# Identity products in TensorE's idle stretches, and one thread's wide keys and values early, in a planned four-block transformer kernel

## The chip, the cores and the metric

The kernel runs on one core of one Trainium2 chip. The metric is the time of one execution on the device in microseconds (us). All data are fp32. A core has TensorE (PE: matrix products and transposes, results into PSUM), VectorE (DVE), ScalarE (ACT), GpSimd (POOL) and SyncE (SP), which here only issues DMAs. In a trace one fp32 product is two instructions, each with its own load of the stationary operand; a transpose is one.

## The reference

Eight sequences of 128 tokens with 256 features, `x`, pass through four blocks. `ctx` has the same shape and is what the cross attentions look at. Cut to what matters:

```python
# block 0: 16 heads of 16 features, keys and values from ctx, mask over keys
x = x + attn(LN(x), ctx) @ cproj_w + cproj_b
x = x + gelu(LN(x) @ fc_w + fc_b) @ proj_w + proj_b              # 256 -> 1024 -> 256
# block 1: queries from x, keys and values from ctx and x together (256 keys)
a = attn(x, concat(ctx, x)) @ out_w + out_b + x
x = x + gelu(RMS(a) @ mlp_w1 + mlp_b1) @ mlp_w2 + mlp_b2
# block 2, twice: 16 wide heads of 128 features, one learned extra key and value
for i in (1, 2):
    q, k, v = LN(x) @ wq, ctx @ wk, ctx @ wv                      # 256 -> 2048 each
    x = x + softmax([q k', q bias_k'] / sqrt(128)) @ [v, bias_v] @ wo + bo
x = x + gelu(LN(x) @ w_fc1 + b_fc1) @ w_fc2 + b_fc2
# block 3: self attention with a causal mask, cross attention to ctx, MLP
x = x + attn(LN(x), LN(x)) @ w_ao + b_ao
x = x + attn(LN(x), ctx) @ w_co + b_co
x = x + gelu(LN(x) @ w1 + b1) @ w2 + b2
```

Only block 2's keys and values are wide, and they depend on nothing but `ctx` and weights.

## The kernel before, in words

**Threads.** The eight sequences are worked on in four threads, T0 to T3, of two sequences (256 tokens) each. Each runs through the four blocks by itself: ten stages with weights of their own, namely a0, m0, a1, m1 (blocks 0 and 1; a is attention, m is MLP), the two wide attentions, m2, then a4, a5, m3 (block 3). T2 starts when T0 has left m1 (`front_done`), T3 when T1 has left it and T0 has left the wide attentions (`wide_done`). So at the beginning only T0 and T1 run.

**Planner.** The instruction order of every engine is written by a planner, class `Plan`, when the program is built. Every step is a Python generator started by `spawn` with an urgency (lower goes first). A step asks for an engine with `op(engine, function)`, waits for an `Event`, or takes buffers from a `Slots` counter. `Plan.run` keeps a clock of its own: when it holds an engine to be free, `_choose` takes the waiting request of lowest urgency, runs its function (which records the instructions) and adds a modelled duration from `_weight`. On the chip each engine runs its list in that order, and semaphores make it wait for what it really needs. `Clock` models TensorE's clock: windows of 3413 ns, full speed in the next window if the last was busy enough, half if not. Every instruction is recorded by the wrapper `Engine`, so all of them bear one line in a trace, and groups are told apart by their tiles.

**Names of tiles.** `mm` (2 banks), `tl` (2 banks) and `sc` (4 banks) are PSUM: `mm` takes projections and MLPs, `tl` transposes, wide scores and weighted values, `sc` the scores of narrow heads. `w` is a weight tile of 512 KB (11 buffers, at most four in use by a thread), `kb` a 128x256 tile for wide keys, wide queries and hidden MLP units (20), `vw` wide values (4), `bv` the wide value bias (2), `t` softmax weights, `xn` a normalised input, `hT` its transpose, `q`, `k`, `v`, `mp`, `tm`, `attnT` the parts of narrow attention, `ident` the 128x128 identity.

**Wide attention.** `wide_attention(T, i)` takes the norm, then the four groups of four heads one after the other with `group(T, i, hg, hT, hT_in)`. In a group, `keys` projects `ctx` into four `kb` tiles (two blocks of four products of 128x256, evicted by ACT or DVE with a bias), `queries` does the same with the normalised input, `values` projects each sequence of `ctx` into a `vw` tile (two products of 128x512, evicted by DVE with the bias `bv`, which `value_bias` makes from two DMAs of 256 KB and a subtraction on POOL). Then, for each sequence, come scores, softmax and the product with `wo` (`after_scores`).

**Weights.** `loader(T)` asks for a thread's weights in the fixed order of `weight_list` as its four slots come free; the DMAs are issued by SP in the order in which the planner reaches them.

**Urgencies.** Each stage has a constant, and each thread three offsets added to it, one for the stages before the wide attentions, one for those, one for the stages after: `LATE = [(0.0, 0.0, 2.3), (3.0, 0.1, 4.5), (2.3, 1.3, 2.6), (1.3, 0.8, 2.3)]`.

Of the kernel before, what the change touches and what calls it, by code (L numbers as in the profile page):

```python
# [58 lines left out]

class Event:  # L60
# [14 lines left out]
class Plan:  # L75
# [12 lines left out]
    def __init__(self):  # L88
        self.now = 0
        self.seq = 0  # L90
        self.events = []
        self.asked = []
        self.until = {e: 0 for e in self.SEEN}
        self.weight, self.shared, self.wrote = 0, False, []
        self.both_until = {"DVE": 0, "POOL": 0}
        self.clock = Clock()
        self.log = []
        self.table = None
        self.dma_until = 0
        self.live = {}  # L100
# [76 lines left out]
    def run(self):  # L177
        self.now = max(self.until.values())
        while self.events or self.asked:
# [3 lines left out]
            for eng in self.until:  # L183
                if self.until[eng] <= self.now:
                    got = self._choose(eng)
                    if got:
                        _, a, (_, ns, f, lat, table), load = got
                        self.asked.remove(a)
                        self.weight, self.shared, self.wrote = ns, False, []
# [6 lines left out]
                        self.log.append((eng, self.now, end - self.now, f.__qualname__.replace("four_blocks.<locals>.", "").replace("<locals>.", "")))  # L196
# [14 lines left out]
class Clock:  # L211
# [4 lines left out]
    def __init__(self):  # L216
        self.t, self.busy, self.fast = 0.0, 0.0, False
        self.end = self.W

# [9 lines left out]
    def work(self, start, ns):  # L229
        self._go(start, False)  # L230
        while ns > 1e-6:
            speed = 1.0 if self.fast else 0.5
            d = min(self.end - self.t, ns / speed)
            self._go(self.t + d, True)
            ns -= d * speed
        return self.t


def _weight(eng, name, args, kw):
# [6 lines left out]
    if eng == "PE":  # L246
# [8 lines left out]
        return max(224, 1.685 * cols), False  # L255
# [29 lines left out]
class Engine:  # L285
# [5 lines left out]
    def __getattr__(self, name):  # L291
        f = getattr(self._eng, name)

        def call(*args, **kw):
# [3 lines left out]
            if eng != "PE" and any(x.tensor is y.tensor and x.offset == y.offset for x in aps[1:] for y in plan.wrote):  # L298
# [4 lines left out]
            plan.shared |= both  # L303
            return f(*args, **kw)  # L304
# [21 lines left out]
def four_blocks(ctx: ExitStack, tc: tile.TileContext, a: dict, out: bass.AP):  # L326
# [40 lines left out]


# [47 lines left out]
    class Thread:  # L416
        def __init__(self, h, b0, nb):
# [10 lines left out]
            self.late = 0.0  # L428

# [42 lines left out]
    def loader(T):  # L472
        for name, shape, pieces in weight_list():
# [7 lines left out]
    def all_then(evs, then):  # L481
        for e in evs:
            yield e
        plan.set(then)
# [32 lines left out]
    def each(*rs):  # L517

        for e in [spawn(asks(r), 0.0) for r in rs]:
# [137 lines left out]
    def product(ops, take):  # L657
# [5 lines left out]
        return spawn(taken(p, take), 0.0, Plan.SEEN["PE"])  # L663
# [6 lines left out]
    def mlp(T, name, src, e, w, b, b1, func, table, adds, to):  # L670
        hT, hT_in = yield from normed(T, src, e, w, b, adds, 2.0 + T.late)
# [22 lines left out]
        yield spawn(first(), 3.0 + T.late)  # L694
# [11 lines left out]
        yield spawn(second(), 3.0 + T.late)  # L706
# [45 lines left out]
    def attention(T, name, norm, ns, own_keys, scale, qb, kb_, vb, mask_of, masks, to):  # L752
# [7 lines left out]
        hT, hT_in = yield from normed(T, *norm, 1.0 + late)  # L760
# [8 lines left out]
        between = spawn(fill(v, 1.0 if by_key else 0.0), 2.0 + late)  # L769
# [11 lines left out]
        biases_in = spawn(cols_then(biases), 2.0 + late)  # L781
        mask_in = spawn(mask_of(mask, k, hs, ks, biases_in), 2.0 + late)
# [63 lines left out]
        k_in = [spawn(keys(s, *src), 2.0 + late) for s, src in enumerate(sources)]  # L846
        yield weight(T, f"{name}qo")
        q_in = spawn(queries(), 1.5 + late)
        v_in = [spawn(values_of(s, *src), 2.5 + late) for s, src in enumerate(sources)]
# [17 lines left out]
        yield spawn(out(), 1.0 + late)  # L867

    def by_keys(T, ns, scale, mask, masks, q, k, v, v_in, vb, attnT):
# [4 lines left out]
        def item(b, c0, n):  # L874
# [94 lines left out]
            e1 = spawn(even_part(1), 0.5 + late)  # L969
# [18 lines left out]
        for b in range(T.nb):  # L988
            for c0 in range(0, NC, 2 // ns):
                done.append(spawn(item(b, c0, 2 // ns), 0.5 + late))  # L990
# [3 lines left out]
    def by_pairs(T, ns, scale, mask, masks, q, k, v, v_in, vb, attnT):  # L994
# [4 lines left out]
        def item(b):  # L999
# [17 lines left out]
            soft = [spawn(softmax(s[:, r], b, r, mn, sm, ts), 1.0 + late) for r in range(4)]  # L1017
# [26 lines left out]
        def values(b, soft, ts, turn, next_turn):  # L1044
# [3 lines left out]
            for r in range(4):  # L1048
# [14 lines left out]
                evs.append(spawn(out_of(pt, pts[:, r]), 1.0 + late, Plan.SEEN["PE"]))  # L1063
# [23 lines left out]
        for b in range(T.nb):  # L1087
            soft, ts = yield from item(b)
            nxt = Event()
            done.append(spawn(values(b, soft, ts, turn, nxt), 0.5 + late))  # L1090
# [25 lines left out]
    def wide_attention(T, i):  # L1116
        hT, hT_in = yield from normed(
            T, T.x, 1e-5, f"L2_ln{i}_scale", f"L2_ln{i}_offset", [(T.x, T.x, f"L2_bo{i}")], 0.5)
# [6 lines left out]
    def group(T, i, hg, hT, hT_in):  # L1125

        n = f"l{i}{hg}"
        ks, qs, vs = [], [], []
        bv = new(wpool, [P, 512], "bv", bufs=2)
        bv_in = spawn(value_bias(bv, i, hg), 1.0)  # L1130
        sb = new(act, [P, 4], "sb", bufs=6)
        late, nb, nt = T.late, T.nb, T.nt
        v_in = [Event() for _ in range(nb)]

        def keys():
# [17 lines left out]
            drop(T)  # L1153
            for e in ends:
                yield e

        def queries():
            yield weight(T, n + "q")
            yield hT_in
            s = P ** -0.5  # L1160
            yield op("POOL", lambda: nc.gpsimd.tensor_scalar(
                sb, col(f"L2_bq{i}", 4 * hg, 4), s, None, ALU.mult))
            ends = []
            for m in range(0, 4, 2):
                yield (kb_slots, 2)
                two = [kb(), kb()]
                qs.extend(two)

                def take(p, two=two, m=m):
                    b = col(f"L2_bq{i}", 4 * hg + m, 2)  # L1170
                    yield from each(*(either(
                        lambda j=j: nc.scalar.activation(
                            two[j][:, :nt], p[:, j * nt : (j + 1) * nt], AF.Identity, bias=sb[:, m + j : m + j + 1], scale=s),
                        lambda j=j: nc.vector.tensor_scalar(
                            two[j][:, :nt], p[:, j * nt : (j + 1) * nt], b[:, j : j + 1], s, ALU.add, ALU.mult),
                    ) for j in range(2)))
                ends.append((yield from product(proj(T.w[n + "q"], hT, (m, m + 1)), take)))
# [231 lines left out]
```

## Time and profile before

| | |
|---|---|
| median of 3 runs | 1224.16 us (1221.81 to 1225.23) |
| profiled execution | 1224.51 us |
| its span, first to last instruction | 1222.7 us |
| TensorE busy | 1146.0 us, 94% of the span |
| DVE, ACT, POOL busy | 759.8, 563.1, 341.9 us |
| mean granted TensorE clock | 0.975 |
| moved by DMA | 145.57 MB |

The profile gives each engine's busy time, then the span in 40 slices of 30.6 us in which a digit is the busy share in tenths, with the TensorE clock that was granted (in tenths of full speed), then DMA queues, the chain of work that ended last, and the costliest groups of instructions. A line of windows gives the same for any stretch of time; a line of the timeline gives a start, a busy time, the group, and in brackets the idle time before it and what ended it. A row's mean duration is longer than the pitch at which such instructions follow each other, since products are pipelined.

### The profile page before, as it was taken

The page shows a single profiled execution, that of the slowest core. Times are in us where ns is not written, and L with a number is a line of the kernel's source. Part 1 is how long each engine was busy: PE and PEld are TensorE (multiplying, and loading weights), DVE is VectorE, ACT ScalarE, POOL GpSimd, SP SyncE. Part 2 cuts the span into 40 slices and gives each one's busy share as a digit, 9 for nine tenths or more (in the row PEclk, how much of TensorE's full clock was granted, in tenths as well). Part 3 has the DMA queues.
Part 4 walks back from the last instruction along what each step waited for, and adds up shares of the span by engine and source line. Part 5 has one row for each costly group of instructions (what it writes and reads, how often), then busy time and mean ns, then how long its engine had stood idle before and what let it go on. Part 6 is the DMA issues. An engine that isn't in the chain of part 4 may idle for free.

```text
span 1222.7 us, 21753 instructions
## 1 busy us (share of the span) xinstructions
PE 1146.0 (94%) x8224; PEld 936.9 (77%) x8224; DVE 759.8 (62%) x1955; ACT 563.1 (46%) x1418; POOL 341.9 (28%) x397
## 2 busy tenths in 40 slices
PE   6699799999999999999999999999999999989868
PEld 4577577787877877868877888888887888877647
DVE  6665668625773546758668564444637756788771
ACT  4244445344533334527346443335333634968652
POOL 3021111111112212116424120221212522676660
PEclk9699899999999999999999999999999999989879
DMA  9133142444434443553434325454436245321400
GB/s 296 42 92 106 36 130 90 138 123 138 118 120 140 146 150 101 147 171 99 121 92 136 106 91 187 141 159 139 143 121 179 75 149 156 111 81 44 131 1 18
DMA packets 107320, 145.57 MB, mean 119 GB/s; under 512 B 6736, under 2 KB 66256, under 8 KB 107216
## 3 DMA queue, kind: packets, MB, share of 16 engines
q1 hardware_dynamic: 107216, 144.18, 38.4%
q8 instruction: 65, 1.06, 0.3%
q14 instruction: 39, 0.32, 0.1%
HBM read 143.11 MB, written 1.05 MB: 118 GB/s over the span
## 4 chain that ended last, share of the span: by engine, by line
PE 78%; DVE 11%; ACT 6%; DMA 3%; issue 1%; POOL 1%; SPq 0%; ACTq 0%; DVEq 0%; POOLq 0%
PE mm L304 56%; PE tl L304 17%; PE sc L304 5%; DVE t L304 1%; ACT t L304 1%; ACT L304 1%; DVE mp L304 1%; DVE rz L304 1%; DMA w<-in_L_k_w 1%; DVE q L304 1%; DVE tm L304 1%; ACT pt L304 1%; DVE mn L304 1%; DVE x L304 1%; ACT q L304 1%
## 5 line engine op out<-in xcount | busy, mean ns | idle before, releaser
L304 PE MATMUL mm<-hT,w 128*128 128x256 f32 x1216 | 289.8, 385 | 9.3 <-ACT kb L304 2.0
L304 PEld LDWEIGHTS mm<-hT,w 128*128 128x128 f32 x1216 | 226.7, 192 | 47.5 <-issue 5.9
L304 POOL TENSOR_TENSOR t<-t,sm 128x512 f32<-128x512 f32 x128 | 131.8, 1043 | 337.9 <-DVE sm L304 206.5
L304 PE MATMUL mm<-ctxT,w 128*128 128x256 f32 x608 | 145.4, 384 | 9.6 <-DMA w<-in_L_k_w 9.5
L304 PE MATMUL mm<-w,ctxT 128*128 128x512 f32 (+1 forms) x352 | 144.0, 539 | 1.9 <-ACT kb L304 0.9
L304 PEld LDWEIGHTS mm<-ctxT,w 128*128 128x128 f32 x608 | 113.0, 192 | 26.7 <-issue 9.8
L304 DVE TENSOR_TENSOR x<-mm,x 128x256 f32<-128x256 f32 (+1 forms) x96 | 49.0, 510 | 131.2 <-PE mm L304 130.9
L304 POOL TENSOR_TENSOR x<-x,row 128x512 f32<-128x512 f32 x40 | 50.8, 1270 | 272.3 <-ACT xn L304 180.4
L304 PE MATMUL mm<-w,at 128*128 128x256 f32 x512 | 121.5, 381 | 1.3 <-PE mm L304 1.0
L304 PE MATMUL mm<-w,kb 128*128 128x256 f32 x512 | 117.8, 380 | 0.0
L304 PEld LDWEIGHTS mm<-w,at 128*128 128x128 f32 x512 | 95.0, 190 | 19.0 <-issue 3.7
L304 PEld LDWEIGHTS mm<-w,kb 128*128 128x128 f32 x512 | 95.5, 190 | 14.1 <-issue 1.4
L304 ACT ACTIVATE t<-t,mn 128x128 f32<-128x128 f32 x256 | 99.0, 391 | 8.4 <-DVE mn L304 6.5
L304 PE MATMUL tl<-ident,t 128*128 128x128 f32 x512 | 79.9, 287 | 16.6 <-POOL t L304 9.8
L304 PEld LDWEIGHTS mm<-w,ctxT 128*128 128x128 f32 x352 | 63.4, 192 | 39.3 <-issue 32.1
L304 POOL TENSOR_TENSOR t<-t,mask 128x512 f32<-128x512 f32 x64 | 80.4, 1280 | 46.3 <-DVE t L304 44.2
L304 PEld LDWEIGHTS tl<-ident,t 128*128 128x128 f32 x512 | 63.3, 147 | 34.2 <-POOL t L304 18.7
L304 ACT ACTIVATE t<-t 128x516 f32<-128x516 f32 x64 | 40.5, 633 | 101.9 <-DVE t L304 101.8
L304 ACT ACTIVATE kb<-mm,cols 128x256 f32<-128x256 f32 x128 | 53.2, 471 | 71.2 <-PE mm L304 70.9
L304 ACT ACTIVATE at<-tl,cols 128x128 f32<-128x128 f32 x204 | 58.2, 368 | 54.8 <-PE tl L304 54.5
L304 POOL TENSOR_TENSOR bv<-bv,bb 128x512 f32<-128x512 f32 x32 | 40.6, 1270 | 115.2 <-DMA bb<-in_L_bias_v 94.6
L304 DVE TENSOR_SCALAR kb<-mm,cols 128x256 f32<-128x256 f32 x61 | 28.9, 481 | 66.6 <-ACT kb L304 64.8
(117 smaller groups left out, 1798.6 us busy)
## 6 DMA issues: line engine op xcount, KB each, us to landing
w<-in_L_wk SPq DMA_DIRECT2D x32, 512.0 KB, 4.3
w<-in_L_wq SPq DMA_DIRECT2D x32, 512.0 KB, 3.7
w<-in_L_wv SPq DMA_DIRECT2D x32, 512.0 KB, 3.7
w<-in_L_wo SPq DMA_DIRECT2D x32, 512.0 KB, 3.4
w<-in_L_mlp_w SPq DMA_DIRECT2D x16, 512.0 KB, 3.9
bv<-in_L_bv SPq DMA_DIRECT2D x32, 256.0 KB, 4.6
bb<-in_L_bias_v SPq DMA_DIRECT2D x32, 256.0 KB, 5.7
w<-in_L_w_fc SPq DMA_DIRECT2D x16, 512.0 KB, 3.9
```

The source lines that it names most:

```text
L304: return f(*args, **kw)
```

## The change

**Identity products.** When the planner finds TensorE free with no request for it, and its model says that the clock is slow or that TensorE was busy for less than 0.55 of the last 3413 ns, it records one product of the identity with itself (128x128) into a free `mm` or else `tl` bank. Nothing reads the result. It can do so again as soon as that product has ended in its model.

**Early keys and values.** `keys` and `values` move out of `group` into a function of their own, `keys_values`. For T0, the groups (1, 0) and (1, 1), that is eight heads of the first wide attention, are started at the beginning of `blocks`, with an offset of their own; `group` picks up the result. `loader` takes their four weights after the first two of T0's list. In a group that isn't early, the queries are now started before the keys, and the values are started when the keys' requests are done.

**Urgencies and prices.** The stages' constants move into a table `U` with new values, and `LATE` now has ten offsets for each thread, one for each stage. The planner's price of a product goes from `max(224, 1.685 n)` to `max(225, 1.7 n)` ns for n columns. It now finds by name, not by object, that an instruction reads what the one before it on its engine wrote, and then adds the delay that it already had for that. `count` and `log` are bookkeeping.

By the built order of instructions, 64 identity products are in the new program: 17 before the first other product, 6 and 4 in the first attentions of T0 and T1, 9 between scores of T1's a1 and the transposes of T0's norm for m1, 12 before the transposes of T0's first wide norm, and 16 among the last stages (2, 2, 9 and 3). The other products are the same in number.

```diff
+WARM = True
+AHEAD = [[(1, 0), (1, 1)], [], [], []]
+U = {'take': 0.33, 'taken': -1, 'norm': 0.36, 'mask': 1.35, 'k': 2.41, 'q': 1.92, 'v': 2.5, 'by key': 0.5, 'softmax': 2.4, 'weights': 0.74, 'pairs': 0.3, 'out': 0.94, 'mlp norm': 0.75, 'mlp 1': 3.6, 'mlp 2': 2.28, 'wide norm': -1, 'wide k': 3.49, 'wide q': 4.0, 'wide v': 4.5, 'wide s': 1.19, 'wide': -0.42, 'ahead': 2.48}
+LATE = [(2.3, -0.18, 0.84, -0.88, 1.83, -0.17, 2.53, 1.2, 3.66, 1.59), (7.76, 6.61, 5.49, 5.66, 1.7, 0.2, 4.52, 3.1, 7.31, 7.88), (1.86, 2.79, 2.79, -0.1, 2.14, -1, 4.58, 4.78, 5.62, 1.93), (0.03, 1.63, -0.02, 0.92, 0.05, 2.99, -1, 0.16, -1, -1)]
...
                     got = self._choose(eng)
+                    if not got and eng == "PE" and self.idle_work and (self.events or self.asked):
+                        self.weight = 0
+                        if self.clock.lazy(self.now) and self.idle_work():
+                            self.until[eng] = self._end(eng)
...
+    def lazy(self, now):
+
+        self._go(now, False)
+        self.spans = [(a, b) for a, b in self.spans if b > now - self.W]
+        return not self.fast or sum(b - max(a, now - self.W) for a, b in self.spans) < 0.55 * self.W
...
-        return max(224, 1.685 * cols), False
+        return max(225, 1.7 * cols), False
...
-            if eng != "PE" and any(x.tensor is y.tensor and x.offset == y.offset for x in aps[1:] for y in plan.wrote):
+            if eng != "PE" and any(x.tensor.name == y.tensor.name and x.offset == y.offset for x in aps[1:] for y in plan.wrote):
...
+    def idle_work():
+
+        for slots, tag in ((mm, "mm"), (tl, "tl")):
+            if slots.free:
+                nc.tensor.matmul(bank(tag)[:, :P], lhsT=ident, rhs=ident, start=True, stop=True)
+                return True
...
     def loader(T):
-        for name, shape, pieces in weight_list():
+        names = list(weight_list())
+        first = {f"l{i}{hg}{x}" for i, hg in AHEAD[T.h] for x in "kv"}
+        ahead = [x for x in names if x[0] in first]
+        names = [x for x in names if x[0] not in first]
+        for name, shape, pieces in names[:2] + ahead + names[2:]:
...
-        k_in, q_in = spawn(keys(), 4.0 + late), spawn(queries(), 4.0 + late)
+        k_in = spawn(keys(), U["wide k"] + step_back)
+        spawn(all_then([k_in], None, lambda: spawn(values(), U["wide v"] + step_back)), 0)
+        return ks, vs, k_in, v_in
...
+        q_in = spawn(queries(), U["wide q"] + late)
+        ks, vs, k_in, v_in = T.ahead.pop((i, hg), None) or keys_values(T, i, hg, late)
         yield k_in
-        spawn(values(), 4.5 + late)
         yield q_in
...
+        for i, hg in AHEAD[h]:
+            T.ahead[i, hg] = keys_values(T, i, hg, LATE[h][0] + U["ahead"])
...
+    plan.idle_work = idle_work if WARM else None
```

## The prediction

> **What bounds the kernel now.** I read the page first, for the engine that is full and where it isn't, then windows over the span, then TensorE's timeline in the windows that stick out. T0 to T3 are the four threads.
>
> ```profile
> span 1222.7 us, 21753 instructions
> PE 1146.0 (94%) x8224; PEld 936.9 (77%) x8224; DVE 759.8 (62%) x1955; ACT 563.1 (46%) x1418; POOL 341.9 (28%) x397
> ...
> PE   6699799999999999999999999999999999989868
> ...
> PEclk9699899999999999999999999999999999989879
> ...
> PE 78%; DVE 11%; ACT 6%; DMA 3%; issue 1%; POOL 1%; SPq 0%; ACTq 0%; DVEq 0%; POOLq 0%
> ```
>
> TensorE is busy 1146.0 of 1222.7 us and carries 78% of the chain of waits. The slices that are not 9 lie in the first five and the last five, and the granted clock dips in the same ones. The windows give their size:
>
> ```profile
> 0.00:176.00 176.00, 142.78 (x1330) 113.47 (x1330) 108.61 (x313) 73.23 (x123) 28.48 (x59) 0.91 0.38 119
> 176.00:1101.00 925.00, 905.59 (x6087) 743.43 (x6088) 577.55 (x1457) 420.11 (x1047) 252.82 (x281) 1.00 0.42 128
> 1101.00:1222.70 121.70, 97.67 (x809) 80.04 (x807) 73.62 (x185) 69.74 (x249) 60.58 (x58) 0.90 0.15 48
> ...
> 30.00:56.00 26.00, 16.25 (x208) 13.51 (x208) 15.24 (x25) 5.51 (x6) 0.00 (x0) 0.61 0.09 32
> 138.00:152.00 14.00, 9.41 (x56) 7.15 (x54) 5.99 (x20) 4.51 (x5) 0.00 (x0) 0.63 0.02 5
> 1083.00:1092.00 9.00, 5.31 (x34) 4.23 (x36) 8.58 (x30) 7.11 (x26) 7.11 (x9) 0.84 0.59 175
> 1146.00:1152.00 6.00, 2.28 (x12) 1.67 (x12) 4.93 (x19) 3.97 (x15) 3.25 (x4) 0.88 0.99 321
> 1166.00:1186.00 20.00, 8.82 (x63) 6.82 (x64) 15.79 (x40) 14.30 (x67) 15.88 (x15) 0.57 0.00 1
> ```
>
> Columns: window, length, TensorE busy, weight loads, DVE, ACT, POOL, granted clock, DMA share, GB/s. TensorE idles 33.2 us in the front (0 to 176), 19.4 in the middle, 24.0 at the end: 76.6 in all. The middle is 98% full, so work taken out of it comes off the span one for one. Front and end are chains of single threads, with TensorE waiting on DVE, ACT and POOL.
>
> The cold clock is the second loss. Busy time times one minus the clock gives 16.25 x 0.39 = 6.3 us in 30 to 56, 9.41 x 0.37 = 3.5 in 138 to 152, 8.82 x 0.43 = 3.8 in 1166 to 1186; some 2.9 each behind 1090 and 1150, and 1.8 at the start: 21 us. Useful work at full clock is then about 1125 us; all else is loss.
>
> ```profile
> 35.14 1.94 PE L304 MATMUL tl<-pt,v 128*32 128x128 f32 x32 [1.99 <-ACT pt L304]
> 37.01 2.09 PE L304 MATMUL sc<-q,k 32*128 32x128 f32 x32
> ...
> 60.84 0.66 PE L304 MATMUL tl<-ident,xn 128*128 128x128 f32 x4
> 61.43 1.17 PE L304 MATMUL sc<-q,k 32*128 32x128 f32 x32
> ...
> 167.13 3.72 PE L304 MATMUL mm<-ctxT,w 128*128 128x256 f32 x16
> ...
> 216.40 3.60 PE L304 MATMUL mm<-w,ctxT 128*128 128x512 f32 x8
> ```
>
> The same block of scores takes 2.09 us at 37 and 1.17 at 61: cold against warm. The last two rows price the wide work: a block of keys (8 instructions) 1.73 us by its pitch, a block of values (4 instructions of 512) 1.80.
>
> **1. Wide keys and values early: the largest term.** Two groups of four heads have two blocks of keys and two of values each: 4 x 1.73 + 4 x 1.80 = 14.1 us. In the changed order all eight stand between T0's first key projection and the end of its first core, the stretch of 20 to 50 us. What they displace: at the transposes of T0's first wide norm (176.05 us before), the old order has 122.5 us of useful products behind it and the new one 133.1, by these pitches. The difference is 10.6 and not 14.1, because two key blocks already stood there.
>
> Does the chain of T0 and T1 get longer? Walking the new order with the trace's durations, the blocks sit between scores and the products that wait for the exponentials (1.89 us on ACT). Two blocks (3.6 us) in a gap of 1.9 cost about 1.7 each time, twice; the warm clock gives back 0.9 per block of scores and of weighted values, of which there are seven. DVE takes four value evictions (0.69 each) and about half of the eight key evictions (0.48). Two of the former stand among T1's first maxima, which hold that chain: 1.4 us. I come out level within 2 us at T0's first output product.
>
> What moves with it. SP has the two bias loads (256 KB each) ahead of the first weights: 0.5 MB at the 331 to 351 GB/s of 10 to 30 us is 1.5 us more before the first product (8.30 before). That is covered: the first real product is now the normalised input's transpose, ready at 9.8 anyway. T1's input comes about 3 us later (1.0 MB more ahead of it), under wide blocks. T0's MLP weights fall behind the second group's; the DMA share is 0.09 from 30 to 56 and they are needed near 60. POOL gets two subtractions of 1.27 us where it is empty. Eight of 20 key buffers and all four value buffers stay taken until T0's wide scores; nobody else asks for the latter, and one MLP (8) still fits. If that cover fails, a late load stalls TensorE by some 5 us.
>
> **2. Products of the identity.** There are 64: 17 before the first work, 10 in the first attentions, 9 where T0's second MLP waits for its norm, 12 before T0's wide norm, 16 in the end. No row shows one; nearest is the wide score product, 66.4 us for 512 instructions, two to a product, so 0.26 us each and 16.6 for all. Those at the start cost nothing (until 9.8 us TensorE has no input). The other 47 are 12.2 us, between zero in real gaps and 12.2 if each stands before ready work. I take 2.
>
> The gain is the warm clock. In 138 to 152 the chain is pure latency with a cold 2.09 us of scores and a cold 5.58 us MLP block inside (1.17 and about 3.7 warm): 2.8, say 3 us off the chain. In 30 to 56 I have spent the gain above.
>
> Here the Trainium skill speaks against it. Its page "TensorE: Matmul & The Clock Gate" (What's actually happening) lets the clock fall after an idle window of about 3.4 us. By that rule the products in half-busy stretches buy nothing. The trace disagrees: from 34 to 44 the clock stays at 0.50 with TensorE busy 6.9 of 10 us, and it fell at 31 with no 3.4 us of idleness before it. By the rule the 3 us would be nearer 0; I follow the trace.
>
> The same page (Part 4: PE-mode transpose) says that transposes don't count as busy for the clock. From 1172 to 1184 TensorE runs almost only transposes, cold; no row tells whether they count. If they don't, the 12 products in that hole are too few: the end keeps its 3.8 us of cold loss, without them it may lose it. I book half.
>
> **3. New urgencies everywhere.** One offset per thread and stage, and new prices, reorder the 925 us in the middle. In a stage 98% full there is little to win and more to lose. The new order has no identity product between T0's wide norm and the last 130 us, so it expects no half-empty window there. Two holes late in the old middle (1083 to 1092: 3.7 us idle, and 1146 to 1152: 3.7) have two products each in the new one and look smaller. I take -4; bounds -12 and +12.
>
> **4. The end.** From the transposes of T3's last self-attention norm (1101.35) to the end, the old order has 95.5 us of useful work in 121.4, the new one 90.7. T3's last two attentions took 48.9 us each there, though the second had only 27 us of products beside it, so it is a chain; I expect 48 + 48 + 21 = 117: -4, bounds 0 and -10.
>
> **Sum.** Front: -10.6 (fill) and -3 (clock), so -14; middle -4; end -4; identity products +2. Total -20. The profiled execution took 1224.51 us, 0.35 over the median of 1224.16 and 1.8 over its span, so this carries over: 1204.
>
> **The rivals.** (a) The front's fill is not free: T0's and T1's chain grows by what is put into it (late w, DVE evictions). For: DVE is busy 27.5 of 40 us from 20 to 60, and TensorE waits for its maxima at 49.62. Against: ACT and POOL are nearly empty there. Front -4, rest -3: 1217.
>
> (b) Slower: a pile-up on DVE, ACT and POOL in the last third. T1 is put back far: its third MLP comes at 864 us of products instead of 742, so T1, T2 and T3 do their last attentions together. Each softmax of four heads takes 2.3 us on POOL (1.28 + 1.04) and as much on ACT (four times 0.39 + 0.19). The hole of 1166 to 1186 is of that kind and costs 11.2 + 3.8 = 15 us. If two more open, +30 on 1204 gives 1234; from 1.3 such holes it is slower. Against: the six attentions spread over 212 us of products, before over 231; POOL needs 111 of either.
>
> (c) The middle improves as well, with shorter evictions before each reader: -12 there and -8 at the end: 1190.
>
> (d) Clock unchanged by 64 products and the order's gain lost in the middle: 1222.
>
> **How the numbers follow.** Forecast 0.62; (a) 0.16; (b) 0.07; (c) 0.11; (d) 0.04. A measurement tells 0.3% (3.7 us) from no change. Faster by more: the forecast, (a), (c), less a little for their spread: 0.88; within: 0.05; slower: 0.07. The range reaches into (a) and (c): 1187 to 1219.
>
> **What would show it.** Right: windows 30 to 56 and 138 to 152 at a clock near 1, TensorE over 85% busy in the first, T0's first wide-norm transposes near 173 us, middle idle under 20 us, T3's last part 115 to 119 us. Wrong: those transposes after 180, or waits for ctxT's w in the first 50 us (a); a new slice below 9 between 900 and 1150 us with DVE and POOL full (b).

## The result, and the profile after

| | before | after |
|---|---|---|
| median of nine runs | 1222.87 us (1220.25 to 1226.00) | 1211.76 us (1206.27 to 1218.14) |
| ratio | 1 | 0.9912, 95% interval 0.9890 to 0.9934 |
| profiled execution | 1224.51 us | 1218.14 us |
| its span | 1222.7 us | 1216.3 us |
| granted clock of the runs | 0.972 to 0.979 | 0.986 to 0.996 |

The kernel is 0.88% faster, 11.1 us; the forecast was 1204 us, 20 us faster, with a range of 1187 to 1219 that holds the measured 1211.76. The profiled execution is the slowest of the nine, so its trace shows the changed kernel at its worst: 6.4 us above its own median. The nine times follow the clock: 1206.27 us at 0.996, 1210.30 at 0.993, 1214.06 at 0.989, 1218.14 at 0.986.

From the page of the changed kernel:

```profile
span 1216.3 us, 21992 instructions
...
PE   7998999999999999999999999999999999998988
...
PEclk9899998999999999999999999999999999999999
...
PE 74%; DVE 16%; ACT 4%; DMA 3%; issue 1%; POOL 1%; SPq 0%; ACTq 0%; POOLq 0%; DVEq 0%
```

In the first line of digits the holes of the front (6, 6 and a 7 in the fifth slice before) and of the end are mostly filled; in the second, the seventh slice, 182 to 213 us, has a dip in the clock that it did not have. TensorE's share of the chain fell from 78% to 74%, DVE's rose from 11% to 16%. The same windows as before (length, TensorE, weight loads, DVE, ACT, POOL, granted clock, DMA share, GB/s):

```profile
0.00:176.00 176.00, 158.53 (x1428) 125.23 (x1429) 105.58 (x298) 73.75 (x126) 28.86 (x58) 0.95 0.42 131
176.00:1101.00 925.00, 901.68 (x6088) 741.55 (x6090) 565.13 (x1425) 415.51 (x1047) 248.31 (x275) 0.99 0.42 126
1101.00:1216.30 115.30, 102.89 (x846) 83.70 (x838) 76.54 (x206) 71.03 (x255) 63.02 (x60) 0.98 0.17 54
30.00:56.00 26.00, 24.72 (x252) 17.40 (x252) 17.62 (x39) 9.99 (x16) 1.27 (x1) 0.91 0.66 217
138.00:152.00 14.00, 11.21 (x99) 8.48 (x100) 11.95 (x32) 3.26 (x9) 1.52 (x5) 0.96 0.24 75
```

Both windows that were to fill did: 24.72 of 26 us at a clock of 0.91, and 11.21 of 14 at 0.96. Yet T0's first wide norm, which has 10.6 us more work behind it, did not come earlier; it came 11.7 us later, at 187.73 us. Before, it stood here:

```profile
176.05 0.63 PE L304 MATMUL tl<-ident,xn 128*128 128x128 f32 x4 [0.29 <-DVE tm L304]
```

To see what each stretch lost, the useful work must be taken out of its length. Between the two traces it is the difference of the counts of products: with the prediction's pitches (0.216 us for an instruction of 256 columns, 0.45 for one of 512; as estimates from the traces 0.117 for a transpose, 0.031 for a small product of weighted values) the new order has 10.6 us more in front of T0's first wide norm, 14.4 us less in the middle and 3.8 us more at the end. The end has 20 more instructions of 256 columns and 4 more transposes, and 32 fewer of the small ones.

| stretch | length before | after | change | of it useful work | change of the loss | forecast |
|---|---|---|---|---|---|---|
| start to T0's first wide-norm transposes | 176.05 | 187.73 | +11.7 | +10.6 | +1.1 | -14 |
| from there to the transposes of T3's last self-attention norm | 925.3 | 915.2 | -10.1 | -14.4 | +4.3 | -4 |
| from there to the end | 121.4 | 113.3 | -8.0 | +3.8 | -11.8 | see step 4 |

In the middle TensorE idles 23.3 us (925.00 less 901.68), before 19.4; at the end 12.4 us (115.30 less 102.89), before 24.0. What shrank most at the end is the hole in T3's last attention, of which these are the waits before, and the longest one after:

```profile
1172.59 2.11 PE L304 MATMUL tl<-ident,t 128*128 128x128 f32 x8 [6.61 <-POOL t L304]
1178.96 1.08 PE L304 MATMUL tl<-ident,t 128*128 128x128 f32 x4 [4.25 <-DVE sm L304]
```

```profile
1175.45 1.94 PE L329 MATMUL tl<-pt,v 128*32 128x128 f32 x32 [2.96 <-DVE pt L329]
```

The middle and the end are taken up again below. The first question is where the front's 14 us went. The trace names two places. The first, in SP's timeline (start, busy, group):

```profile
8.00 0.40 SPq L415 DMA_DIRECT2D row<-in_rows  x1
10.32 9.05 SPq L415 DMA_DIRECT2D bb<-in_L_bias_v  x2
19.41 0.43 SPq L415 DMA_DIRECT2D mask<-in_mask_b  x1
```

and in SP's waits up to 40 us (what for, us in total, times, longest):

```profile
SPq L415 <- DMA bb<-in_L_bias_v: 6.4, 1, 6.4
...
SPq L415 <- POOL bv L329: 2.0, 1, 2.0
```

`value_bias` has one buffer `bb` (`bufs=1`). With two groups early, the second `bb` load has to wait until the first has landed (6.4 us) and POOL has subtracted it (2.0). SP issues in order, so it stands there (the row of both loads lasts 9.05 us), and T1's mask, input, context and weights stand behind: the mask is issued at 19.41 us, before the change at 6.65. What that does, in the timelines of DVE and TensorE, first before and then after:

```profile
17.62 0.28 DVE L304 TENSOR_SCALAR mask<-mask 128x256 f32<-128x256 uint8 x1
```

```profile
24.42 1.17 PE L304 MATMUL sc<-k,q 32*128 32x128 f32 x32
```

```profile
24.16 0.29 DVE L329 TENSOR_SCALAR mask<-mask 128x256 f32<-128x256 uint8 x1 [7.60 <-DMA mask<-in_mask_b]
...
27.74 2.35 DVE L329 TENSOR_REDUCE mp<-sc 128x8 f32<-128x1024 f32 x2
```

```profile
26.80 2.60 PE L329 MATMUL mm<-ctxT,w 128*128 128x256 f32 x8 [3.43 <-DVE kb L329]
30.23 2.09 PE L329 MATMUL sc<-k,q 32*128 32x128 f32 x32 [0.83 <-DVE ry L329]
```

DVE works in order too: T0's maxima (21.92 us before) stand behind T1's mask, and T0's second block of scores starts at 30.23 and not 24.42. TensorE's wait is put down to DVE's `kb` eviction, which itself only stood behind the mask. The second place, ACT's and TensorE's rows around T0's first wide norm:

```profile
180.54 0.60 ACT L329 ACTIVATE xn<-x,rz,ry 128x256 f32<-128x256 f32 x1 [1.26 <-DVE rz L329]
```

```profile
180.84 7.10 PE L329 MATMUL mm<-ident 128*128 128x128 f32 x18 [1.97 <-DVE v L329]
187.73 1.06 PE L329 MATMUL tl<-ident,xn 128*128 128x128 f32 x4
188.72 2.09 PE L329 MATMUL sc<-q,k 32*128 32x128 f32 x32
```

The normalised input is there at 181.14, but nine products of the identity stand ahead of its transposes, on a clock that fell at 181.66: 0.79 us each, so the transposes come 6.6 us later, behind work that nothing reads. (Without the nine, part of these 6.6 us stays as another wait; see below.)

### The profile page after: what moved, and what is told of

It is laid out like the page before. It is cut to its first block, busy times and chain, and to the rows that moved or that the text cites. A ratio compares the mean times of both kernels' runs of the same rounds, so it can differ in the third digit from the quotient of the medians.

```text
span 1216.3 us, 21992 instructions
## 1 busy us (share of the span) xinstructions
PE 1163.1 (96%) x8352; PEld 950.5 (78%) x8352; DVE 747.2 (61%) x1927; ACT 560.3 (46%) x1428; POOL 340.2 (28%) x393
## 4 chain that ended last, share of the span: by engine, by line
PE 74%; DVE 16%; ACT 4%; DMA 3%; issue 1%; POOL 1%; SPq 0%; ACTq 0%; POOLq 0%; DVEq 0%
PE mm L329 54%; PE tl L329 15%; PE sc L329 5%; DVE t L329 2%; DVE tm L329 2%; DVE rz L329 1%; DVE mx L329 1%; DVE mp L329 1%; ACT t L329 1%; DVE q L329 1%; ACT q L329 1%; DVE rv L329 1%; DVE sm L329 1%; POOL t L329 1%; DVE st L329 1%
## 5 line engine op out<-in xcount | busy, mean ns | idle before, releaser
L329 PE MATMUL mm<-hT,w 128*128 128x256 f32 x1216 | 285.7, 383 | 5.5 <-ACT hT L329 1.9
L329 PE MATMUL tl<-ident,t 128*128 128x128 f32 x512 | 75.6, 277 | 6.2 <-POOL t L329 2.1
L329 PEld LDWEIGHTS tl<-ident,t 128*128 128x128 f32 x512 | 60.0, 142 | 24.6 <-issue 8.9
L329 ACT ACTIVATE kb<-mm,sb 128x256 f32<-128x256 f32 x72 | 32.7, 471 | 91.4 <-PE mm L329 90.6
L329 ACT ACTIVATE at<-tl,cols 128x128 f32<-128x128 f32 x188 | 53.4, 369 | 44.2 <-PE tl L329 44.1
L329 PEld LDWEIGHTS tl<-kb,kb 128*128 128x128 f32 x512 | 64.3, 192 | 10.3 <-issue 7.7
```

## The experiments

Theory: the change's gain in the front was eaten by these two places. Rivals: the products' clock is the whole gain, so that taking any away makes it slower; and the delay of T0's chain comes from the wide blocks and their evictions themselves, so that moving loads changes nothing. A third stands beside both: the profiled execution is the slowest of nine, and cold clock windows of its own lengthen the front whatever the order. Ratios are to runs of the kernel before on the same chip, 95% intervals in brackets; a difference of ratios of 0.001 is 1.2 us.

| kernel | ratio | median us |
|---|---|---|
| the changed kernel | 0.9912 (0.9890 to 0.9934) | 1211.76 |
| no products of the identity | 0.9938 (0.9916 to 0.9960) | 1216.80 |
| without the nine | 0.9870 (0.9848 to 0.9891) | 1208.47 |
| early loads issued later | 0.9884 (0.9858 to 0.9910) | 1209.50 |
| both | 0.9891 (0.9871 to 0.9910) | 1210.53 |
| loads sorted, without the nine | 0.9865 (0.9843 to 0.9887) | 1207.55 |
| second `bb` in a buffer of its own | 0.9867 (0.9841 to 0.9894) | 1209.18 |
| the same, without the nine | 0.9849 (0.9828 to 0.9870) | 1206.26 |
| loads sorted, own buffer, without the nine | 0.9852 (0.9830 to 0.9875) | 1206.53 |
| before, with products only | 0.9954 (0.9938 to 0.9971) | 1217.73 |
| before, with early groups only | 1.0317 (1.0291 to 1.0344) | 1263.99 |
| new urgencies only | 1.0325 (1.0302 to 1.0347) | 1262.72 |
| new urgencies and products | 1.0265 (1.0245 to 1.0285) | 1255.30 |

**No products.** `idle_work` charges the planner as before and records nothing, so that all other instructions keep their order.

```diff
+                plan.weight += 225
+                return True
-                nc.tensor.matmul(bank(tag)[:, :P], lhsT=ident, rhs=ident, start=True, stop=True)
```

> The changed kernel in its own order, with none of the 64 products of the identity. Theory 1 (the products do little as a whole: they win some clock in the first half-empty stretches and give it back where nine of them run cold before T0's first wide norm): 1209 to 1213 us, T0's first wide-norm transposes (187.7 us with the products) between 182 and 188, the MLP block near 152 us cold again at about 5.6 us, and the end 2 to 4 us longer. Theory 2 (the products' clock is the whole gain of the change): 1219 us or more.

It came between the theories, at 1216.80 us: all 64 together are worth 0.0026, some 3 us, which the overlap of the intervals does not secure. The transposes came at 186.48 us, no later than with the products, and the MLP block behind 152 us took 3.72 us, not 5.6 as expected: in this execution the clock happened to be up there. From T3's last self-attention norm to the end it took 1.3 us longer and not 2 to 4.

```profile
155.57 3.72 PE L329 MATMUL mm<-hT,w 128*128 128x256 f32 x16
...
186.48 1.08 PE L329 MATMUL tl<-ident,xn 128*128 128x128 f32 x4 [5.71 <-ACT k L329]
```

**Without the nine.** Products 40 to 48 are left out in the same way.

```diff
+                made[0] += 1
+                if 39 < made[0] <= 48:
+                    plan.weight += 225
+                    return True
```

> The changed kernel in its own order, without the nine products of the identity that stand directly before T0's first wide-norm transposes; the other 55 stay. Theory 1 (these nine run cold, 0.79 us each, ahead of transposes that are ready at about 181 us): the transposes move from 187.7 to about 182 us and the whole is 1206 to 1208 us. Theory 2 (the clock that they hold up is worth what they cost): 1212 us or more, the transposes earlier but the blocks behind them cold for as long.

1208.47 us, 0.0042 or 5 us better than the changed kernel, as theory 1 said, though the two intervals just touch. The transposes:

```profile
179.38 1.09 PE L329 MATMUL tl<-ident,xn 128*128 128x128 f32 x4 [5.48 <-ACT k L329]
180.40 2.09 PE L329 MATMUL sc<-q,k 32*128 32x128 f32 x32
```

8.3 us earlier than 187.73, of which 5.0 were there ahead of the nine (the order and the single `bb` are the same up to there, but this execution starts warmer) and 3.4 came at them: the transposes start 5.5 us after the product before them, with the nine 8.9 us. The scores behind are cold, 2.09 us, but so they were with the nine: these nine did not hold the clock up. In the two traces in which they ran cold (this change and the own buffer below) the clock stays at 0.50 for 10.24 us there, in the traces without them for 6.83 or 3.41 us. Against the kernel without any product this one is 0.0068 or 8 us better, and these two intervals are apart: the other 55 products are worth 8 us.

**Early loads later.** SP issues the early `bv`, `bb` and the first wide `w` behind T1's mask, input, context and first weights.

```diff
-        e = spawn(load(bv, a[f"L2_bv{i}"][:, s].partition_broadcast(P), 256), 0)
+        e = spawn(load(bv, a[f"L2_bv{i}"][:, s].partition_broadcast(P), 256, True), 0)
...
+            if wide and early[0]:
+                held.append((dst, src))
+                return
             nc.sync.dma_start(out=dst, in_=src)
+            if flush:
+                early[0] = False
+                for d, s in held:
+                    nc.sync.dma_start(out=d, in_=s)
```

> The changed kernel with one thing moved: SP issues the early bias loads and the first early weights of wide keys and values behind T1's mask, T1's x, its context and the first weights, not ahead of them. The order of all other instructions stays. Theory 1 (DVE, which works in order, waits at 24 us for T1's mask and holds T0's maxima and evictions behind it): the 3.4 us wait of TensorE at 26.8 us goes, the first real weights are there at about 9.5 us and not 11.2, T0's second block of scores comes 3 to 5 us earlier than 30.2 us, and the whole is 1205 to 1208 us. Theory 2 (the delay comes from the wide blocks and their evictions themselves, whatever the loads): no change within 1 us of 1212, and the weights for the wide blocks, loaded later, become a new wait.

The mask came earlier (DVE's row for it moved from 24.16 to 13.4 us), the first weights were there at 9.76 us, T0's second scores at 26.24. But TensorE now waits for the wide weights:

```profile
17.97 2.97 PE L329 MATMUL mm<-ctxT,w 128*128 128x256 f32 x8 [2.45 <-DMA w<-in_L_wk]
...
35.91 1.97 PE L329 MATMUL mm<-ctxT,w 128*128 128x256 f32 x8 [1.67 <-DMA w<-in_L_wk]
```

The ratio of 0.9884 is 3 us better, with overlapping intervals. In this profile the clock is 1.00 from 149 to 1160 us, and the nine still took 4.86 us:

```profile
175.81 4.86 PE L329 MATMUL mm<-ident 128*128 128x128 f32 x18 [1.96 <-DVE v L329]
180.51 0.60 PE L329 MATMUL tl<-ident,xn 128*128 128x128 f32 x4
```

That is 0.54 us each at full clock, where nine others (at 145.38 us in the changed kernel) took 0.29. The trace tells why: here the weight load of every one but the first waits for the product before it (8 waits, 2.0 us; in the changed kernel's cold nine 8 waits, 2.7 us), and at 145.38 none does. So the nine are slow for two reasons, the clock and a wait for each other. Why they wait for each other, whether for a PSUM bank, was not tried.

**Both**, that is these two diffs together.

> Both edits together: early bias and wide loads issued behind T1's mask and input, and the nine products before T0's first wide norm left out. Theory 1 (two separate losses): the two gains add, 1200 to 1203 us. Theory 2 (one of the two is no loss): no better than the better one of the two alone, 1206 to 1212 us.

1210.53 us: the two did not add. T0's maxima were 4.1 us ahead of the kernel without the nine at 30 us and 0.9 at 58; the waits for `w` had taken it back. Moving the loads was the wrong cure, and I had the wrong cause: I had put the mask's delay down to the bytes ahead of it.

**Loads sorted.** SP's first 31 loads in the order of their readers: T0's weights, T1's mask and input, first wide weights, T1's context and weights, the biases, the second wide weights, T2's and T3's inputs; without the nine. Loads of a kind are held and issued behind the one named:

```diff
+            if hold in held:
+                held[hold].append((dst, src))
+                return
             nc.sync.dma_start(out=dst, in_=src)
+            for key in then:
+                for d, s in held.pop(key, ()):
+                    nc.sync.dma_start(out=d, in_=s)
...
+                hold = "wide"
+                if name == "l11v":
+                    then = ("x",)
```

> The changed kernel without the nine products before T0's first wide norm, and with SP's first 31 loads sorted by when they are read: first weights of T0, T1's mask and x, first wide weights, T1's context and weights, then the four bias loads, the second group's wide weights, and only then T2's and T3's inputs. Theory 1 (in the run with late loads the 5 us won by T1's mask were given back because the second group's weights of wide keys, 28th in SP's queue, came 2.2 us late at 33 us): both waits go, and the whole is 1203 to 1206 us. Theory 2 (what is won before 40 us is lost again to chain waits behind it): 1207 to 1211 us, as without the nine products alone.

1207.55 us, theory 2's number. The waits for weights were gone and a third engine stood still. POOL's, DVE's and TensorE's timelines:

```profile
26.54 1.26 POOL L329 TENSOR_TENSOR bv<-bv,bb 128x512 f32<-128x512 f32 x1 [5.06 <-DMA bb<-in_L_bias_v]
```

```profile
28.70 1.27 DVE L329 SCALAR_TENSOR_TENSOR k<-mm,hs,k 128x256 f32<-128x256 f32 x3 [4.78 <-POOL k L329]
```

```profile
30.07 3.75 PE L329 MATMUL mm<-w,ctxT 128*128 128x512 f32 x4 [4.16 <-issue]
```

POOL waits for the second bias, T1's key on POOL stands behind that, DVE's evictions behind the key, TensorE behind them. The second bias is late because SP stands at it for its buffer here as well (8.67 us for the two `bb` rows): the single `bb` is behind both.

**A buffer of its own for the second `bb`.** Nothing else moves; it lands in one of the `vw` tiles, which are empty then.

```diff
-        bb = new(wpool, [P, 512], "bb", bufs=1)
+        biased[0] += 1
+        bb = new(act, [P, 512], "vw", bufs=4) if biased[0] == 2 else new(wpool, [P, 512], "bb", bufs=1)
```

> The changed kernel with one buffer more: the second early bias lands in a tile of its own (one of the four wide value buffers, empty then) and not in the single bb, which it had to wait for. Order and bytes stay. Theory 1 (SP, which works in order, stands 9.05 us at the second bb because of its one buffer, and T1's mask and weights stand behind it): that row of SP shrinks below 1.5 us, T1's mask is there before 16 us and not at 24, T0's second block of scores starts near 26 us and not at 30.2, and the whole is 1206 to 1209 us. Theory 2 (the DMA engines are what holds the loads back, so they come as late without the stop): mask still after 21 us, 1211 us or more.

SP's, DVE's and TensorE's timelines:

```profile
10.58 0.33 SPq L415 DMA_DIRECT2D vw<-in_L_bias_v  x1
11.34 0.33 SPq L415 DMA_DIRECT2D mask<-in_mask_b  x1
```

```profile
17.49 1.22 DVE L329 TENSOR_SCALAR mask<-mask 128x256 f32<-128x256 uint8 x1 [3.02 <-DMA mask<-in_mask_b]
```

```profile
25.00 1.17 PE L329 MATMUL sc<-k,q 32*128 32x128 f32 x32 [1.43 <-DVE ry L329]
...
172.53 6.92 PE L329 MATMUL mm<-ident 128*128 128x128 f32 x18 [1.96 <-DVE v L329]
179.25 1.06 PE L329 MATMUL tl<-ident,xn 128*128 128x128 f32 x4
```

With the same bytes in the same order, the mask is issued at 11.34 and not 19.41 us, T0's second scores start 5.2 us earlier, and the nine are reached 8.3 us earlier. Part of that is the clock: the first weights ran warm here. Against the run without the nine, which starts as warm and has the single `bb`, the second scores are 4.5 us earlier, and the products just ahead of T0's wide norm, at 178 us in the changed kernel, 3.3 us:

```profile
29.54 1.52 PE L329 MATMUL sc<-k,q 32*128 32x128 f32 x32 [0.38 <-DVE ry L329]
```

The mask is read at 17.49, not before 16 as expected, so 3 us of transfers remain. The ratio of 0.9867 is 5.5 us better than the change's; its interval just touches the change's. The nine still cost 6.92 us here. The same buffer with the diff that leaves out the nine:

> The buffer of its own for the second early bias, and the nine products of the identity before T0's first wide norm left out. Theory 1 (both are separate losses of the front): 1201 to 1205 us, T0's first wide-norm transposes before 178 us. Theory 2 (what is won before 40 us is lost behind it, in chains that wait for other things): 1206 to 1209 us, as without the nine products alone.

1206.26 us, a little over the 1205 that theory 1 allowed. Its interval (to 0.9870) lies below the change's (from 0.9890): the two removals together are secured, 7.7 us. The transposes came at 177.88 us with the same work behind them, before 178 as expected:

```profile
177.88 1.09 PE L329 MATMUL tl<-ident,xn 128*128 128x128 f32 x4 [5.49 <-ACT k L329]
```

Lost in the front, counted with the prediction's sums of useful work: 177.88 - 133.1 = 44.8 us, 8.8 less than before (176.05 - 122.5) and 9.8 less than in the changed kernel (187.73 - 133.1). The chain runs 6.0 to 6.5 us ahead of the changed kernel's from 38 to 178 us (the buffer, with what each execution's clock adds) and 9.8 ahead at the transposes (the nine).

The buffer with the sorted loads, without the nine:

> The kernel with SP's loads sorted by when they are read and without the nine products, with the second early bias in a buffer of its own. Theory 1 (in the sorted run GpSimd waited 5.1 us for the second bias, which itself waited for the one bb, and DVE 4.8 us for GpSimd): both waits go, TensorE's 4.2 us hole before 30 us too, and the whole is 1201 to 1205 us. Theory 2 (as before, the gain is lost behind 40 us): 1206 to 1208 us.

1206.53 us: no better than that, though the front is (transposes at 175.27, T1's mask read at 13.25). What the order of loads adds on top is not told from nothing.

**The parts alone.** First the products in the old order, the kernel before with `lazy`, `idle_work` and the lines in `run` that call it:

```diff
+    plan.idle_work = idle_work
     spawn(inputs(), 0)
```

> The kernel before, with the rule for products of the identity alone (it places 64 again, in the old order's own holes; urgencies, early groups and charged prices are the old ones). Theory 1 (the products win clock in half-empty stretches, net some 3 us in the changed order by the run without them, more in the old order because it has more cold time): 1215 to 1219 us, a granted clock above the 0.975 of before. Theory 2 (they only fit the new order): 1222 us or more.

1217.73 us, 0.46% faster: theory 1 (its trace has 66 products of the identity). Two windows and the first real product of that kernel, against 16.25 us of TensorE at a clock of 0.61, 9.41 at 0.63, and 3.75 us of a cold first block at 8.30:

```profile
30.00:56.00 26.00, 19.13 (x266) 15.46 (x264) 17.77 (x33) 6.69 (x9) 0.00 (x0) 0.80 0.17 52
138.00:152.00 14.00, 11.73 (x103) 9.91 (x104) 6.18 (x23) 6.55 (x10) 0.00 (x0) 0.88 0.17 54
```

```profile
7.55 1.97 PE L318 MATMUL mm<-ctxT,w 128*128 128x256 f32 x8 [1.57 <-DMA w<-in_L_k_w]
```

Then the early groups and the urgencies, each without the rest, and the urgencies with products. The first has the old urgencies and prices and `WARM = False`, the second both lines below, the third only that of `AHEAD`:

```diff
-WARM = True
-AHEAD = [[(1, 0), (1, 1)], [], [], []]
+WARM = False
+AHEAD = [[], [], [], []]
```

> The early groups alone: old urgencies and prices, no products of the identity, and T0's first two groups of wide keys and values early (without the early groups this source gives the order of before on every engine). Theory 1 (the fill is worth something by itself, whatever the urgencies): 1213 to 1219 us, 30 to 56 us fuller, T0's first wide-norm transposes within 3 us of 176. Theory 2 (the fill pays only with urgencies set for it, as the two runs without early groups would suggest of the urgencies): 1222 us or more.

> The changed kernel with neither early groups nor products of the identity: what is left of the change are the new urgencies and prices. Theory 1 (these alone give little; they were set for an order with the early groups): 1224 to 1232 us, slower than the run with products only. Theory 2 (the urgencies are the main part of the gain): 1212 to 1216 us.

> The changed kernel with the list of early groups empty: products of the identity and new urgencies stay, and the plan is made anew with them (103 products, since there are more holes). Theory 1 (the early groups fill front holes that nothing else fills): 1220 to 1228 us, with 30 to 56 us half empty of useful work as before. Theory 2 (the early groups only move work): 1212 us as the changed kernel.

1263.99, 1262.72 and 1255.30 us: the second and third are far slower than either theory allowed, and the first fell on the side of theory 2 (1222 or more), which had not named such a size. In the first, the transposes that can be T0's first wide norm come at 188.3 us or later, not within 3 us of 176. Windows of the early groups alone, then of the urgencies alone:

```profile
176.00:1101.00 925.00, 890.66 (x5885) 729.88 (x5879) 548.34 (x1397) 408.11 (x971) 230.17 (x259) 0.99 0.42 125
1101.00:1260.20 159.20, 127.35 (x1053) 102.92 (x1051) 99.85 (x252) 94.10 (x334) 82.85 (x80) 0.91 0.18 53
```

```profile
176.00:1101.00 925.00, 890.52 (x6036) 726.23 (x6035) 554.17 (x1392) 413.61 (x1049) 246.64 (x273) 0.99 0.41 125
1101.00:1258.10 157.10, 123.04 (x854) 98.43 (x852) 77.72 (x214) 79.44 (x269) 62.16 (x60) 0.90 0.20 59
```

TensorE idles 34 us in the middle (19.4 before) and 32 and 34 at the end (24.0 before), and the last part is 157 to 159 us long instead of 122. With both but without products it is 0.9938. So early groups and urgencies can't be priced apart: each alone costs 39 or 40 us, together they bring 8. Which of the urgencies carries this, and which thread comes late for it, was not followed further. Products in this plan, 103 of them, bring 0.6% again (1.0325 to 1.0265).

## Why the prediction was right, and where not

**Step 1, the early groups: the largest term, and it failed.** The fill itself came as forecast: both windows are full, and 10.6 us more work stands before T0's wide norm. The failed sentence is that T1's input would come about 3 us later, "1.0 MB more ahead of it", under wide blocks. I costed SP's queue by bytes over bandwidth, and the mask was issued 12.8 us later. What held it was a buffer: the second `bb` waits for the first one's landing and its reader, 8.4 us, and SP's queue waits with it. The kernel's text says `bufs=1`; before the change the loads of `bb` were 7.3 us or more apart, and no such row of SP took over 1.45 us. The wide blocks did not cover it, because the wait was not TensorE's: it went from SP to DVE's in-order list and came back to T0.

Forecast -14 for the front, +1.1 in the profile. Not all of the difference is the buffer. Without the nine the front is 179.38 - 133.1 = 46.3, -7.2; with the own buffer as well -8.8; and sorted loads on top give 175.27 - 133.1 = 42.2, -11.3. Of the 9.8 us between +1.1 and -8.8 the traces put some 5 on the cold clock of the profiled execution, 3.4 on the nine, and the rest, 1.5, on the buffer, or 3.3 if the run with the nine and the own buffer is taken; one trace each can't settle that. Secured by times is only the removal of both, 7.7 us.

Rival (a), the fill not free, had the right sign ("late w, DVE evictions"; transposes after 180; TensorE waited 1.29 us for `w` at 11.21), and its 1217 was 5.2 us off where the forecast's 1204 was 7.8. Its mechanism, a chain longer by what is put into it, is not what the runs show in the main: the same work in the same order is faster once the buffer is there.

**Step 2, the products: net about right, both terms too small.** I booked a cost of 2 and a gain of 3, half of the end's cold loss aside. By the medians the nine alone cost 5 us (0.9912 to 0.9870, intervals that touch), and the other 55 bring 8. The cost was mis-sized because 0.26 us is the price of a warm product that waits for nothing. The nine run cold and wait for each other, 0.79 us each; with the wait alone it is 0.54.

On the clock, the choice of trace over rule held. The Trainium skill, "TensorE: Matmul & The Clock Gate" (What's actually happening), makes the clock fall after an idle window of about 3.4 us; here it fell in half-busy stretches, and with products in them it was higher (from 30 to 56 us 0.80 in the kernel before with products only, 0.61 in the kernel before). What I left out of that section is that its window runs freely and does not start with the kernel. The trace agrees: cold stretches come in steps of 3.41 us, and executions with the same instructions up to a point catch them at different places. Windows of the changed kernel set on such stretches, the first of them with the window before it, and then the window before the first weights in the run without the nine:

```profile
7.57:10.98 3.41, 1.78 (x11) 1.13 (x10) 3.04 (x16) 2.12 (x5) 2.44 (x7) 1.00 0.96 316
10.98:14.39 3.41, 3.18 (x8) 2.56 (x9) 0.12 (x1) 1.46 (x4) 0.07 (x1) 0.50 1.02 373
...
181.66:191.90 10.24, 9.84 (x58) 7.23 (x58) 6.49 (x24) 3.94 (x8) 2.17 (x5) 0.50 0.33 66
```

```profile
6.41:9.80 3.39, 2.52 (x17) 1.91 (x15) 3.04 (x19) 1.09 (x2) 2.42 (x9) 1.00 0.89 261
```

The 17 products had brought the clock up in both. In the first, the next window was only half busy (1.78 of 3.41 us), the clock fell at 10.98, and the first weights met it cold (3.54 us). In the second, the window held more of the products (2.52 of 3.39 us busy), the clock stayed, and the same block ran warm (1.97 us at 10.95). The spread of the times rose from 5.8 to 11.9 us over nine runs; that such windows cause it is likely, as the times follow the clock, but not shown.

**Step 3, the urgencies: wrong in the profile.** The middle was to lose 4 us less; it lost 4.3 more, and TensorE idles 23.3 us there, where under 20 was the sign. The nine traces with this order of the useful work (the changed kernel and eight of the runs) take 909.4 to 916.3 us for the stretch, the shortest with a clock of 1.00 throughout, so the change of the loss is -1.5 to +5.4, and none reaches -4. As a part with bounds of 12 either way the term was wrong too: alone the urgencies are +40 us. Constants tuned for a plan are no addend.

**Step 4: the direction right, the work under it wrong.** T3's last part took 113.3 us (forecast 117, sign 115 to 119), 112.4 to 114.9 in all nine traces. The prediction gave the old order 95.5 us of useful work there and the new one 90.7. The counts of products say that the new order has 3.8 us more, so about 86.9 in the old one; the prediction's own window speaks for that as well, with 97.67 us busy at a mean clock of 0.90, which makes an estimate of 88. So its -4 was -8.2 in lost time (34.5 to 26.3), and its four terms make -24 or 1200 and not 1204. Measured -11.8: the holes of 6.61 and 4.25 us have become one of 2.96, and the clock there is 0.98 and not 0.90. The products have a small part in it (1.3 us in the run without any); the rest is left to the order, early groups and urgencies together, and was not taken apart.

**The sum and the rivals.** Rival (b), a pile-up on POOL and DVE, did not come: one slice of 8 between 900 and 1150 us, and the end is where the kernel gained most. Rival (c)'s middle of -12 did not come either, but its -8 for the end is what was measured in time.

So the direction and the range were right, and for other reasons than given: front +1.1, middle +4.3, end -11.8 make -6.4 in the profiled execution, where -14, -4, -8.2 and +2 were forecast. Two of the three stretches went the other way there, and that the range held is in good part luck. The median execution is 4.7 us better still, at a clock of 0.991 and not 0.986.

## What to carry to other kernels

When a load moves forward, count the buffers of its tile before its bytes: a load that waits for a buffer stops every load behind it in its queue (here for 8.4 us), and an in-order engine passes that on to threads that have nothing to do with it. Filler work must be priced at the clock that holds where it stands, with the waits of one piece for the next, and kept off the place just ahead of what the chain waits for. Constants that were tuned together are tested together: here either half alone cost 3.2%, and both brought 0.6%. And compare the work of two orders by counting it in the same stretch of both: here a sum for one of them was off by 8.6 us, twice the term that rested on it.

## What was not expected of the hardware

A product of the identity costs four different times. In the changed kernel's trace such products follow each other every 0.43 us in the first cold stretch (from 1.9 to 7.1 us) and take 0.29 in a warm one (nine in 2.57). Where each waits for the one before it, they take 0.54 at full clock (nine in 4.86) and come every 0.85 us once the clock has fallen. These last stand in a stretch of 10.24 us at a clock of 0.50, of which TensorE's rows fill 9.84; after the 17 at the start, which don't wait for each other, the clock was up at 7.57 us. Whether the waits are the reason was not tried.
